# Convolution-attention hybrid on one core: attention steps at an even rate, layer 0 divided by token, the third convolution on VectorE, an earlier load of x, and the last feed-forward in step

## The chip, the core and the metric

The kernel runs on one core of a Trainium2 chip. The metric is the device time from the first to the last instruction, in microseconds (us). Before the change it is 7679.73 us, the median of three runs (7679.41 to 7688.48). The profile shown here is of an execution with a span of 7673.1 us. The engines are named as in the profile: PE (TensorE matmul) and PEld (its weight loads), DVE (VectorE), ACT (ScalarE), POOL (GpSimd) and SP (SyncE).

## The reference

The input x has 4 images of 128 channels and 64 x 64 = 4096 positions. Everything is fp32. Cut to what matters, this is computed:

```python
# layer 0, per image
e1 = prelu(w1 @ gn(x)); e2 = prelu(w2 @ gn(x)); asm = prelu(wa @ gn(x))      # 64, 64 and 128 channels
x  = x + einsum('nij,ncj->nci', softmax(einsum('nci,ncj->nij', e1, e2), axis=2), asm)
# layer 1, attention over 4096 tokens of 128 numbers, 16 heads of 8
t  = tokens(x); y = ln(t)
q  = qz_ring(y + rx)                      # products of cosines; q is query, key and value at once
c  = softmax(q @ q.T / sqrt(8)) @ q       # per head
x1 = ln(y + c @ w_comb.T + b) * g1 + be1
t  = t + ln(x1 + relu((cos(x1[:8]) * cos(ry)) @ w1.T + b1) @ w2.T + b2) * g2 + be2
# last layer: a recurrence over the tokens after a norm over all of them
W' = batchnorm(ln(t) @ W.T);  y_k = sigmoid(W'_k + y_{k-1} @ V.T);  out = t + y
```

In layer 0 the softmax runs over j, so each position i is divided by a sum of its own. In attention q serves as query and as key, so the score of (i, j) is also that of (j, i).

## The kernel before, in words

The images are worked one after the other. Each has three stages.

**First stage** (`first_stage`, `layer0`, `tokens`). x lies by channel, `xs` of 128 x 4096. After the group norm three 1x1 convolutions make e1, e2 and asmT. The first two are rectified by `prelu` (two Relu passes on ACT, L281 and L282, and one product on DVE, L283), the third one likewise. Then come 8 tiles `ic` of 512 positions i. For each the loop takes the 4096 positions j in 32 groups of 128, two groups (one `jp`) at a time: `scores` makes s (PE, L365), p = exp(s) (ACT, L373) and adds p to `total` (DVE, L378 and L381), and `weigh` multiplies asmT with p into one accumulator (PE, L388). `take` copies the accumulator (L400). `result` sums `total` over partitions with two matmuls by a matrix of ones (L406), inverts the 128 x 512 result (L408), multiplies (L409) and adds to xs (L412, POOL); it also keeps the least and greatest inverse for a check at the end (L416). All this is by channel.

Between two groups the loop calls `meanwhile`. It runs one step of a queue of generators: `tokens(im, i)`, which turns a finished tile of xs by TensorE transposes (L470) into tokens x0 and makes the layer norm x1 and q (L478 to L508), and splits q for the scores (L512 to L521). It also runs steps of the feed-forward of the image before, two tiles at a time. PE, ACT and DVE keep the order in which the program emits their instructions. Transposes and sums of this stage share a pool `ps_tok` of one PSUM bank. The last tile's generator, `tail`, goes on inside attention.

**Second stage** (`attention`). For each of 8 pairs of heads there are 4 blocks of 1024 queries. A step of the inner loop, a *turn*, takes 128 keys `jt`: PE makes scores for two heads (4 matmuls on row tiles, L800), ACT the exp e of 128 x 1024 per head (L809), and PE weighs the turn before with the queries' own values (L679). Since scores are symmetric, only part of the blocks of keys is met: the first two blocks have 24 turns, the other two 16. A turn off the diagonal (`off`) serves twice. Its e is *flipped* by DVE (STREAM_TRANSPOSE in 32 x 32 pieces, L648), ACT sums its rows (`accum_out`), and the flipped copies of four such turns make a group of 16 *mirror steps* (`mirror_step`, L661), whose end goes to `later` by L672 or L674. Of every three turns of a long block two are off the diagonal, of every two in a short block one.

How many mirror steps PE does in a turn is set by a credit. Each turn adds a rate, the sum is capped at 4, and whole steps are taken as far as a group is pending:

```python
credit = min(credit + (3.0 if off else 2.0), 4.0)
if at == 1:
    credit = 4.0
credit -= run_pending(turn, int(credit))
```

A group becomes pending at a turn that `run_flips` sets when it has emitted the group's last flip (L650); `run_flips` holds back a group as long as the group two before it has steps left (L642). The exp tiles e lie in a pool of 6 or, in two of five turns, in the space of xs, which is free then (`exps`). Near the end of the last block xs is needed for the next image: `upcoming` holds the load of x (`load_x`), its statistics and the rest of the norm, started at given turns `at` (L864) and after the last turn (L881). `finish` and its `mirrored` and `result` (L703 to L747) move a block's sums to tokens, mostly by small copies on POOL.

**Third stage** (`third_stage`). The feed-forward of an image (`feed_forward`, 8 tiles of 512 tokens as generators) is interleaved by `in_steps` with the next image's first stage. After the last image it stands alone: each step of the loop takes every active generator one step on, and at most 6 are active.

At the end the recurrence runs over 64 chunks side by side. Each of 64 + 16 steps is two matmuls and a Sigmoid for each of two halves (L1265, L1283, L1290). `add_tokens` adds results to t2 in 16 tiles on DVE after every 16 steps (L1273), and DMAs take the 16 tiles out (L1316).

Of the kernel before, what the change touches and what calls it, by code (L numbers as in the profile page):

```python
# [10 lines left out]
F32 = mybir.dt.float32  # L11
# [15 lines left out]
def kernel(  # L27
# [32 lines left out]
    P = 128  # L60
# [155 lines left out]
    ranges = const.tile([1, 2, N * NIC], F32, tag="ranges", name="ranges")  # L216
# [38 lines left out]

    def transposed(src, name, kind="ps_one"):

        pt = get(kind, name)
        for k in range(TG):
            nc.tensor.transpose(pt[:, ts(k, P)], src[:, k, :], ident)  # L260
        return pt
# [22 lines left out]

    def norm_stats(n, xs):
# [19 lines left out]
    def layer0(n, xs, xh, norm, shifted, done, meanwhile):  # L305
# [23 lines left out]
        for i in range(NIC // 2):  # L329
# [19 lines left out]
            y, z = mid_tile(f"ya{n}_{i}"), mid_tile(f"za{n}_{i}")  # L349
            prelu(asmT[:, ts(i, 2 * IC)].rearrange("p (a b) -> p a b", a=2), pc, y, z, (0.0, 0.0), aa_sb)  # L350
# [51 lines left out]
        def result(ic):  # L402
            total, taken = state.pop(ic), state.pop(("sum", ic))
            sm = get("ps_tok", f"sum{n}_{ic}")
            for j in range(2):
                nc.tensor.matmul(sm, ones, total[:, j, :], start=j == 0, stop=j == 1)  # L406
            inv = half_tile(f"inv{n}_{ic}")
            nc.vector.reciprocal(inv, sm)  # L408
            nc.vector.tensor_tensor(taken, taken, inv, ALU.mult)  # L409

            eng = nc.gpsimd if ic < NIC - 1 else nc.vector
            eng.tensor_tensor(xs[:, ts(ic, IC)], xs[:, ts(ic, IC)], taken, ALU.add)  # L412
            if not shifted:
                for k, op in ((0, ALU.min), (1, ALU.max)):
                    at = n * NIC + ic
                    nc.vector.tensor_reduce(ranges[:, k, at : at + 1], inv[0:1, :], AX.X, op)  # L416
            done(ic)


        before = []  # L420
        for ic in range(NIC):
            for jp in range(0, NP, 2):
                fresh = [(ic, j, scores(ic, j)) for j in (jp, jp + 1)]
                for i in range(2):
                    if before:
# [3 lines left out]
                        elif before[i][0] and before[i][1] == 0:  # L429
                            result(before[i][0] - 1)  # L430
                    meanwhile()
# [4 lines left out]
        result(NIC - 1)  # L436
# [26 lines left out]
    def tokens(im, i):  # L463


        n, q, cols = im["n"], im["q"], ts(i, IC)
        yield
        yield
        yield
        pt = transposed(blocks(im["xs"][:, cols]), f"pt{n}_{i}", "ps_tok")  # L470
        x0 = get("thalf", f"x0_{n}_{i}")
        nc.scalar.copy(x0, pt)
        nc.sync.dma_start(out=im["x0"][:, cols], in_=x0)
        yield
# [952 lines left out]
```

## Time and profile before

The stages of the profiled execution, by the first and last exp of layer 0 and attention (L373, L809) and the first matmul of the recurrence (L1265):

| stage | from (us) | to (us) | length (us) |
|---|---|---|---|
| layer 0, image 0 (with the start) | 0 | 447.1 | 447.1 |
| attention, image 0 | 447.1 | 1764.3 | 1317.2 |
| layer 0, image 1, beside a feed-forward | 1764.3 | 2317.0 | 552.7 |
| attention, image 1 | 2317.0 | 3638.8 | 1321.8 |
| layer 0, image 2, beside a feed-forward | 3638.8 | 4193.4 | 554.6 |
| attention, image 2 | 4193.4 | 5512.6 | 1319.2 |
| layer 0, image 3, beside a feed-forward | 5512.6 | 6063.5 | 550.9 |
| attention, image 3 | 6063.5 | 7384.5 | 1321.0 |
| last feed-forward | 7384.5 | 7568.1 | 183.6 |
| recurrence and output | 7568.1 | 7673.1 | 105.0 |

Attention is 69% of the span. Within it, a long block of image 1 (head pair 4, block 1) goes from 3034.4 to 3084.0 us, the short ones after it to 3116.3 and 3148.3. The groups of the costliest lines:

```profile
L809 ACT ACTIVATE e<-s 128x1024 f32<-128x1024 f32 x3104 | 3068.5, 1027 | 117.1 <-PE s L800 104.8
L648 DVE STREAM_TRANSPOSE t<-e 128x1024 f32<-128x1024 f32 x1872 | 2201.4, 1218 | 653.4 <-ACT e L809 635.8
L661 PE MATMUL misc<-t,mirror 128*32 128x128 f32 x49152 | 1817.9, 278 | 55.4 <-DVE later L672 27.6
```

Each row gives line, engine, operation, output and inputs with their shapes and how often, then the busy time in us and the mean of one in ns, then the engine's idle time just before these instructions and what ended most of it. Matmuls on different row or column tiles of PE overlap, so their busy time is that of their union, and an fp32 matmul is recorded twice.

### The profile page before, as it was taken

The numbers are of one execution on the slowest core, as the hardware profiler recorded it, in microseconds if no ns is written. First come the engines' busy times: TensorE is split into PE (matmuls) and PEld (weight loads), VectorE is DVE, ScalarE is ACT, GpSimd is POOL, SyncE is SP. The second block draws the span as 40 slices with busy tenths as digits, with TensorE's granted clock in tenths as the row PEclk, the third lists the DMA queues.
The fourth block names the chain that finished last, engine by engine and source line by source line (L and its number), as shares of the span: only waits on it lengthen the run. The fifth ranks groups of instructions, "written<-read, shape, count | busy, mean of one in ns | idle before, by whom it ended". The sixth has DMA issues, their size and how long they took to land. (4 is left out here: it accounts for less than half of the span.)

```text
span 7673.1 us, 211342 instructions
## 1 busy us (share of the span) xinstructions
PE 7342.2 (96%) x87566; PEld 3334.3 (43%) x87566; DVE 5561.2 (72%) x7344; ACT 6146.6 (80%) x9493; POOL 2769.3 (36%) x9796
## 2 busy tenths in 40 slices
PE   8999999999999999999899999999999999999976
PEld 3334444444444444444444444444444444444445
DVE  5777777776787777777678777777677877777754
ACT  4479999995448999999444999999844699999964
POOL 1134444343223433343323343444322334444341
PEclk9999999999999999999999999999999999999987
DMA  0010000000111000000011000000001100000012
GB/s 26 25 42 23 25 19 20 19 9 24 33 44 36 25 20 19 23 21 16 18 33 46 32 20 19 22 23 17 17 25 34 52 20 23 23 25 19 11 53 102
DMA packets 81501, 211.92 MB, mean 28 GB/s; under 512 B 8768, under 2 KB 8800, under 8 KB 79760
## 3 DMA queue, kind: packets, MB, share of 16 engines
q1 hardware_dynamic: 77312, 186.68, 7.1%
q8 instruction: 689, 11.29, 0.6%
q10 hardware_dynamic: 2016, 10.49, 0.3%
q14 instruction: 284, 2.33, 0.1%
q0 software_dynamic: 1200, 1.14, 0.1%
HBM read 141.65 MB, written 56.62 MB: 26 GB/s over the span
## 5 line engine op out<-in xcount | busy, mean ns | idle before, releaser
L809 ACT ACTIVATE e<-s 128x1024 f32<-128x1024 f32 x3104 | 3068.5, 1027 | 117.1 <-PE s L800 104.8
L648 DVE STREAM_TRANSPOSE t<-e 128x1024 f32<-128x1024 f32 x1872 | 2201.4, 1218 | 653.4 <-ACT e L809 635.8
L809 ACT ACTIVATE xs<-s 128x1024 f32<-128x1024 f32 x2016 | 1993.0, 1025 | 49.4 <-PE s L800 46.3
L661 PE MATMUL misc<-t,mirror 128*32 128x128 f32 x49152 | 1817.9, 278 | 55.4 <-DVE later L672 27.6
L679 PE MATMUL acc<-e,q_aug 128*32 128x512 f32 x12416 | 1700.9, 595 | 0.0
L648 DVE STREAM_TRANSPOSE t<-xs 128x1024 f32<-128x1024 f32 x1200 | 1413.2, 1218 | 357.8 <-ACT xs L809 346.0
L661 PEld LDWEIGHTS misc<-t,mirror 128*32 128x32 f32 x49152 | 1225.5, 110 | 609.1 <-issue 450.9
L800 PEld LDWEIGHTS s<-queries,keys 32*128 32x128 f32 x10240 | 502.7, 181 | 2154.4 <-issue 1712.8
L715 POOL COPY own<-o 32x36 f32<-32x36 f32 x2048 | 428.6, 209 | 2768.7 <-DVE o L707 2688.8
L800 PE MATMUL s<-queries,keys 32*128 32x512 f32 x10240 | 1312.5, 495 | 11.0 <-ACT e L809 8.8
L679 PE MATMUL acc<-xs,q_aug 128*32 128x512 f32 x8064 | 1148.2, 595 | 0.0
L388 PE MATMUL acc<-p,asmT 128*128 128x512 f32 x2048 | 975.1, 610 | 0.0
L373 ACT ACTIVATE p<-s 128x1024 f32<-128x1024 f32 x512 | 497.0, 1022 | 519.9 <-PE s L365 512.7
L381 DVE TENSOR_TENSOR total<-total,p 128x1024 f32<-128x1024 f32 x448 | 578.0, 1290 | 243.8 <-ACT p L373 220.4
L618 POOL COPY mirror<-q 32x128 f32<-32x128 f32 x2048 | 595.2, 291 | 94.7 <-PE misc L661 6.8
L388 PEld LDWEIGHTS acc<-p,asmT 128*128 128x128 f32 x2048 | 364.2, 191 | 543.8 <-issue 541.5
L365 PE MATMUL s<-e,e 64*128 64x512 f32 x2048 | 531.6, 639 | 4.6 <-ACT p L373 3.0
L734 POOL COPY other<-turned 32x64 f32<-32x64 f32 x2048 | 472.2, 231 | 95.7 <-DVE turned L727 9.9
L679 PEld LDWEIGHTS acc<-e,q_aug 128*32 128x32 f32 x12416 | 390.1, 110 | 91.3 <-issue 42.8
L809 ACT ACTIVATION_READ_ACCUMULATOR e<-s 128x1 f32 x1872 | 388.7, 208 | 0.0
L679 PEld LDWEIGHTS acc<-xs,q_aug 128*32 128x32 f32 x8064 | 259.0, 109 | 112.0 <-issue 55.0
L365 PEld LDWEIGHTS s<-e,e 64*128 64x128 f32 x2048 | 181.9, 192 | 278.2 <-issue 251.1
(237 smaller groups left out, 4901.8 us busy)
## 6 DMA issues: line engine op xcount, KB each, us to landing
keys<-parts_dram SPq DMA_DIRECT2D x256, 256.0 KB
queries<-parts_dram SPq DMA_DIRECT2D x1024, 32.0 KB
fx<-x_dram SPq DMA_DIRECT2D x64, 256.0 KB
x_dram<-x SPq DMA_DIRECT2D x56, 256.0 KB
xs<-in_x_dram SPq DMA_DIRECT2D x16, 512.0 KB
t_dram<-t2T SPq DMA_DIRECT2D x32, 256.0 KB
t2s<-t_dram SPq DMA_DIRECT2D x16, 512.0 KB
parts_dram<-high SPq DMA_DIRECT2D x28, 256.0 KB
```

The costliest lines, as they stand in the source:

```text
L365: nc.tensor.matmul(s[:, j, :], e2[rows, ts(2 * jp + j, P)], e1[rows, ts(ic, IC)], start=True, stop=True,)
L373: nc.scalar.activation(p, s, AF.Exp)
L381: nc.vector.tensor_tensor(state[ic], state[ic], p, ALU.add)
L388: nc.tensor.matmul(state["acc", ic], asmT[:, ts(2 * jp + j, P)], p[:, j, :], start=jp == 0 and j == 0, stop=jp == NP - 1 and j == 1,)
L618: nc.gpsimd.tensor_copy(wv[ts(a, 32), s, :, :, ts(a, D)], own[ts(s, 32)])
L648: nc.vector.transpose(group["e"][h][:, k, :], es[h])
L661: nc.tensor.matmul(state["acc"][ts(2 * h + x, 32), :], state["w"][:, QT * (s // 4) + TG * x + s % 4, h, :], state["e"][h][:, :, ds(IC * x ...
L679: nc.tensor.matmul(it["acc"][ts(2 * h + x, 32), :], it["qa"][:, ds((2 * it["jt"] + h) * V, 32)], it["e"][h][:, ts(x, IC)], start=it["first ...
L715: nc.gpsimd.tensor_copy(own[ts(s, 32), ts(x, 4), h, :], ov[ts(2 * h + x, 32), s, :, 0:V])
L734: nc.gpsimd.tensor_copy(to[ts(k, 32), h], tv[ts(2 * h + x, 32), k])
L800: nc.tensor.matmul(ss[h][:, x, :], keys[jt // QT].bitcast(F32R)[r, cols], queries[b].bitcast(F32R)[r, :], start=True, stop=True,)
L809: nc.scalar.activation(es[h], ss[h].rearrange("p x c -> p (x c)"), AF.Exp, scale=1.0 / math.sqrt(D), accum_out=denom[:, slot, jt, h : h + ...
```

## The change

The change has five parts.

1. *Attention.* The rates at which mirror steps are handed out become those at which they come: 2.9 and 2.2 in long blocks, 2.2 and 1.9 in short ones. A group is pending one turn later. The last tile's generator starts a turn later, one step a turn; as long as it runs, its tokens stand in part of xs, and `exps` uses the pool in place of that part.
2. *Layer 0 by token.* The sums over partitions are made by token and not by channel: the ones matrix is cut to 32 columns, so that a sum of 128 columns goes to each of four column tiles, a DVE transpose and a small inversion give one inverse per token, and the product with the inverse and the addition to x are made in one DVE instruction on the transposed tile. x itself is transposed first. The check of the inverses uses all of them, kept in `inverses`.
3. *Third convolution.* It is rectified by two DVE instructions that read PSUM, in place of two on ACT and one on DVE.
4. *x sooner.* The next image's x is loaded at turn 2 of the last block in place of turn 8; the end of its norm comes after the last mirror steps.
5. *Ends.* In the last feed-forward all 8 tiles are active together, and ACT does their normalisations. In the recurrence the additions follow steps 16, 32, 48, 60 and 64.

The diff, cut to its core:

```diff
+    def normalise_act(dst, src, mv, rstd, n_tiles, name):
+        less = stats.tile([P, n_tiles], F32, tag=f"less{n_tiles}", name=f"less_{name}")
+        nc.vector.scalar_tensor_tensor(less, mv[:, :, 0], -1.0, rstd, ALU.mult, ALU.mult)
+        for k in range(n_tiles):
+            at = slice(k, k + 1)
+            nc.scalar.activation(
+                dst[:, k, :], src[:, k, :], AF.Identity, bias=less[:, at], scale=rstd[:, at]
+            )
...
+    def prelu_vector(dst, src, minus, minus_slope):
+        nc.vector.tensor_scalar(minus, src, 0.0, minus_slope, ALU.min, ALU.mult)
+        nc.vector.scalar_tensor_tensor(dst, src, 0.0, minus, ALU.max, ALU.subtract)
...
-            y, z = mid_tile(f"ya{n}_{i}"), mid_tile(f"za{n}_{i}")
-            prelu(asmT[:, ts(i, 2 * IC)].rearrange("p (a b) -> p a b", a=2), pc, y, z, (0.0, 0.0), aa_sb)
+            to = asmT[:, ts(i, 2 * IC)].rearrange("p (a b) -> p a b", a=2)
+            prelu_vector(to, pc, mid_tile(f"za{n}_{i}"), aa_sb)
...
-        def result(ic):
-            total, taken = state.pop(ic), state.pop(("sum", ic))
-            sm = get("ps_tok", f"sum{n}_{ic}")
-            for j in range(2):
-                nc.tensor.matmul(sm, ones, total[:, j, :], start=j == 0, stop=j == 1)
-            inv = half_tile(f"inv{n}_{ic}")
-            nc.vector.reciprocal(inv, sm)
-            nc.vector.tensor_tensor(taken, taken, inv, ALU.mult)
...
                             take(before[i][0])
-                        elif before[i][0] and before[i][1] == 0:
-                            result(before[i][0] - 1)
-                    meanwhile()
+                            begin(before[i][0], state)
+                    meanwhile(2 if ic == NIC - 1 else 1)
...
-    def tokens(im, i):
+    def tokens(im, i, sums):
...
+        pt = transposed(blocks(im["xs"][:, cols]), f"px{n}_{i}", "ps_tok")
+        x0 = im["xs"][:, cols] if last else get("thalf", f"x0_{n}_{i}")
         nc.scalar.copy(x0, pt)
+        yield
+        total, taken = sums.pop(i), sums.pop(("sum", i))
+        ps = get("ps_tok", f"sum{n}_{i}")[:, 0:P]
+        tv = total.rearrange("p j (k c r) -> p j c k r", c=4, r=32)
+        for j in range(2):
+            for c in range(4):
+                nc.tensor.matmul(
+                    ps[ts(c, 32), :],
+                    ones[:, 0:32],
+                    tv[:, j, c],
...
+                )
+        by_token = small.tile([P, P], F32, tag="sums", name=f"sums{n}_{i}")
+        nc.vector.transpose(by_token, ps)
...
+        nc.vector.reciprocal(inv, by_token.rearrange("p (k r) -> p k r", k=TG)[:, :, 0])
+        if not last:
+            yield
+        pt = transposed(blocks(taken), f"pt{n}_{i}", "ps_tok")
+        if not last:
+            yield
+        for k in range(TG):
+            at = ts(k, P)
+            nc.vector.scalar_tensor_tensor(
+                x0[:, at], pt[:, at], inv[:, k : k + 1], x0[:, at], ALU.mult, ALU.add
+            )
...
-                    pending.append((turn + 1, group["steps"], group["block"]))
+                    pending.append((turn + 2, group["steps"], group["block"]))
...
-            if k < 0 or last:
+            if k < 0 or last or (k and tail):
...
-                    es = exps(name, end_of_all and at >= QT)
+                    es = exps(name, end_of_all and at >= 2)
...
-                    credit = min(credit + (3.0 if off else 2.0), 4.0)
+                    rates = (2.9, 2.2) if len(behind[b]) == 2 else (2.2, 1.9)
+                    credit = min(credit + rates[0 if off else 1], 4.0)
                     if at == 1:
-                        credit = 4.0
+                        credit = max(credit, 3.0)
...
-                    for _ in range(3 if tail and turn == 2 else 1):
-                        if tail and turn > 1 and next(tail, tail) is tail:
-                            tail = None
-                            rest()
-                    if end_of_all and at in (QT, QT + 6) and upcoming:
+                    if tail and turn > 2 and next(tail, tail) is tail:
+                        tail = None
+                        rest()
+                    if end_of_all and at in (2, QT + 6) and upcoming:
...
-        for f in upcoming:
-            f()
         while flips or pending:
             run_flips(TG)
             run_pending(turn + 2, 16)
+        for f in upcoming:
+            f()
...
-            while len(own) > 1:
-                step_first(own)
+            *own, tail = own
+            for g in own:
+                for _ in g:
+                    pass
             while step_late():
                 pass
-        return own.pop()
+            while not next(tail):
+                pass
+        return tail
...
-            step = in_steps(feed_forwards(im, final), 1, 6)
+            step = in_steps(feed_forwards(im, final), 1, NTG)
...
-                if t >= 0 and t % 16 == 15 and t + 1 < L:
-                    add_tokens(t - 15, t + 1)
+                if t + 1 in added:
+                    add_tokens(*added[t + 1])
...
-        add_tokens(L - 16, L)
+        add_tokens(L - 4, L)
```

## Prediction

> **What bounds the kernel now.** I read the page's busy shares, a table of windows cut at the stages, the timeline of TensorE in two attention blocks, and the waits of one attention stage.
>
> The page's engine shares:
> ```profile
> PE 7342.2 (96%) x87566; PEld 3334.3 (43%) x87566; DVE 5561.2 (72%) x7344; ACT 6146.6 (80%) x9493; POOL 2769.3 (36%) x9796
> ```
> PE looks full, but a pipelined PE always does, so the stages decide. Windows (length, then busy us of each engine, granted clock, DMA):
> ```profile
> 27.00:434.00 407.00, 400.50 (x1201) 160.09 (x1202) 272.26 (x358) 182.30 (x192) 47.90 (x57) 1.00 0.06 19
> 1777.00:2308.00 531.00, 497.21 (x1729) 227.04 (x1730) 394.94 (x772) 244.96 (x279) 151.29 (x179) 0.96 0.10 32
> 2317.00:3639.00 1322.00, 1302.84 (x19846) 576.48 (x19846) 979.84 (x1020) 1278.07 (x2054) 525.52 (x2213) 1.00 0.07 23
> 7385.00:7568.00 183.00, 104.33 (x657) 76.57 (x649) 109.35 (x423) 44.39 (x73) 97.06 (x156) 0.68 0.19 69
> ```
> Rows one and two, layer 0 without and with a feed-forward beside it, are PE's. Row three, one of four attentions, has PE and ACT both nearly full: they trade the lead turn by turn. In row four, the last feed-forward, nobody is full: latency.
>
> PE in a long attention block, then in a short one (start, us):
> ```profile
> 2703.01 0.51 PE L800 MATMUL s<-queries,keys 32*128 32x512 f32 x4
> 2703.45 0.86 PE L661 MATMUL misc<-t,mirror 128*32 128x128 f32 x24
> 2704.13 1.04 PE L679 MATMUL acc<-e,q_aug 128*32 128x512 f32 x8
> 2705.10 0.51 PE L800 MATMUL s<-queries,keys 32*128 32x512 f32 x4
> ...
> 2706.77 0.52 PE L800 MATMUL s<-queries,keys 32*128 32x512 f32 x4
> 2707.47 1.08 PE L661 MATMUL misc<-t,mirror 128*32 128x128 f32 x32 [0.18 <-DVE later L672]
> ```
> ```profile
> 3099.80 0.51 PE L800 MATMUL s<-queries,keys 32*128 32x512 f32 x4
> 3100.24 1.08 PE L661 MATMUL misc<-t,mirror 128*32 128x128 f32 x32
> ...
> 3111.89 0.51 PE L800 MATMUL s<-queries,keys 32*128 32x512 f32 x4
> 3112.33 1.27 PE L679 MATMUL acc<-e,q_aug 128*32 128x512 f32 x8
> 3113.53 0.62 PE L800 MATMUL s<-queries,keys 32*128 32x512 f32 x4
> 3114.09 1.63 PE L679 MATMUL acc<-e,q_aug 128*32 128x512 f32 x8
> ```
> A mirror step shows as 8 records. A PE turn is scores 0.44 (2703.01 to 2703.45), k steps 0.03 + 0.218k (3 steps: 0.68), weighing 0.97 (2704.13 to 2705.10): 1.44 + 0.218k, so 2.09 for three steps, 1.87 for two. ACT's floor, from the closest starts of L809, is 1.99 us for a turn with row sums (off the diagonal) and 1.81 without. Long block (24 turns, 16 off, 64 steps): PE 24 x 1.436 + 64 x 0.218 = 48.4, ACT 16 x 1.99 + 8 x 1.81 = 46.3. Short block (16 turns, 8 off, 32 steps): PE 29.9, ACT 30.4. Measured from block start to block start: 49.5 to 49.7 and 32.0 to 32.3. Two losses explain this. Long: a batch's first step starts 0.70 us after its scores instead of 0.44, because the flips it reads are only just done: about 0.27 x 4 batches = 1.1. Short: the 16 steps of a batch run as 4,2,3,2,3,2 and then two turns have none; PE then sets the pace in six turns and ACT in two.
>
> The waits of an attention stage (2381 to 3600) name it:
> ```profile
> PEld misc L661 <- DVE later L672: 14.5, 29, 0.5
> PEld misc L661 <- DVE later L674: 8.0, 16, 0.5
> PE misc L661 <- DVE later L672: 5.4, 29, 0.2
> ```
>
> **What the Trainium skill says.** "Perfetto Trace Analysis", Identifying the Most-Contended Engine: matmul busy share is no measure of nearness to roofline. The trace agrees: PE shows 98.5% in attention although short blocks lose 1.6 us of 32. "TensorE: Matmul & The Clock Gate", Part 3 (row/col tiling): matmuls on different column tiles run at once. The trace agrees: four L661 matmuls, of 272 ns each, start every 0.109 us. "VectorE: DVE Perf Modes", Why PSUM operands drop a tier: fp32 from PSUM runs at 1x. Here L519 (PSUM, 512 elements) takes 687 ns, L230 (SBUF, one source) 422. "ScalarE: Activation LUTs", Table sets: copy, relu and identity are in every set; all 116 table loads here stand at Sin, Exp and Sigmoid lines, none at Copy or Relu.
>
> **The change, part by part.**
>
> *Attention rates and the start one turn later.* Counting the credit rule turn by turn gives, before, 3,3,1,4,3,2 steps per six turns of a long block and the 4,2,3,2,3,2,0,0 above (both are what the trace shows); after, 2,4,2,3,3,2 and nearly all 2. Nothing is added. The batch's first step has 2 us of slack over its flips, so the 1.1 us wait goes; the two-buffer rule of L642 never holds a flip in the count. Long: 49.6 to 48.6 (PE floor plus 0.2). Short: two steps cost PE 1.87, below ACT's mean 1.90, so ACT sets it: 32.1 to 30.7 (floor plus 0.3). Per head pair 2 x 1.0 + 2 x 1.4 = 4.8; x 8 pairs x 4 images = **-154**. Bounds: half of it (-77), or both floors exactly (-176).
>
> *Layer 0 divided by token.* Removed on PE per tile: two full sums, four passes of 0.43 = 1.72, and the transposes of xs with their wait for POOL (L412), 1.00 by the timeline. Added: px and pt, 0.44 each like pq (155.68 to 156.12), and eight 32-column sums, 4 rounds of 0.109 plus switching = 0.55. Net -1.3. DVE loses 3.35 (L408) + 0.69 + 1.33 and gains a transpose (0.25, between L727's 410 ns for twice the size and L674's 258), a reciprocal (0.24 as L741) and four multiply-adds (0.26 to 0.36 each, L674 and L503): -3.5, which hides under PE. New waits: px, sum, pt and pq share the one ps_tok bank; behind a waiting one on PE queue the scores and weighings, and ACT and everything else wait for those. They stand a `meanwhile` (2.8 us) apart, evacuations take 0.3 to 1.5, so without feed-forward nothing waits: image 0 -9. Beside the feed-forward DVE runs late (PE's longest wait for it there is 4.7 us), so I keep -6 for images 1 to 3: **-26** (bounds +20, -42).
>
> *Third convolution.* ACT loses 2 x 1.02 per pair of tiles; DVE goes from 1.29 to two PSUM reads of 1.2 to 1.4. PE takes 3.9 per pair, so it hides; Exp's table load (1.28) moves off the first score: **-4** (bounds +8, -8).
>
> *Tail.* Image 1's first block takes 63.6 against 49.5, the others 58.7, 61.1, 62.8. In image 1 ACT stands 8.3 us at 2332 to 2341 because PE's first mirror step waits for flips that DVE began only at 2323, after reciprocal, product, add and ranges (2316.5 to 2322.6). These leave that place and the step comes one turn later; two Sin/Exp loads and the pq transposes stay, and the shorter exps pool (6 buffers, reused after 3 turns) costs a little: -4 an image, **-16** (bounds +8, -30).
>
> *x sooner.* The load lands by 1756, the statistics run at 1763.8 behind the flips: hidden already. The reordered end lets PE do its last 16 steps during the statistics, but the next convolutions stand behind POOL's chain until 1795 (L741 on DVE's queue), which is not shortened: **0** (bounds +3, -8).
>
> *Last feed-forward.* Six tiles run from 7417 to 7517, the last two alone to 7564. With eight in step the second, half-empty phase goes. DVE gives 96 normalisations (37 us) to ACT for 24 small products, ACT pays 96 x about 0.35 (L1290, L239) on 44 of 183 us busy. 100/6 less 4 of DVE per tile = 12.7; 8 x 12.7 = 102 to 130 us from 7417: **-32** (bounds -12, -48).
>
> *Recurrence.* The output DMA (8.4 MB, about 405 GB/s, 20.7 us) starts after the first final add, 7647.7. Now 16 adds of 12 tokens (about 0.40 each from L1273's 0.50 pitch for 16) start at 7643.1 and hold DVE until 7649.5: **+2**.
>
> Sum: -154 - 26 - 4 - 16 - 32 + 2 = -230; 7679.7 - 230 = **7450**.
>
> **Rivals.**
> - *Half the pacing (a wait takes the other's place).* PE and ACT have only 1.5 turns of scores between them; turns of 4 steps (2.31) may still let ACT idle, or misc wait elsewhere. For: ACT waits for scores 28.7 us per attention now. Against: the sums per six turns are even. -77 instead of -154: 7527.
> - *All floors met.* -176 - 42 - 30 - 48 - 8 + 2: about 7378.
> - *ps_tok stalls PE (slower).* If pt and pq each waited 4.7 us in 24 tiles (+226), layer 0's saving were gone and pacing brought half: 7680 + 226 - 77 - 32 - 16 = 7781. For: PE is in order and DVE is late there. Against: 4.7 us is the longest of eight waits above 1.7 in image 1, and DVE gets 3.5 us lighter per tile.
>
> **How the numbers follow.** As summed 0.70; half pacing 0.17; all floors 0.06; slower 0.07 (a little of it ends within 0.2%). 7385 to 7550 leaves out the stalls and the best end. Faster 0.92, same 0.02, slower 0.06.
>
> **What would show it.** Block starts 48.4 to 48.8 and 30.4 to 31.0 apart; no L672 wait before L661; layer-0 tiles of image 0 at 46.3 instead of 47.55 us; last feed-forward 140 to 165 us; output 2 us later. Wrong if short blocks stay at 32, if PE waits for ps_tok (L260, after a DVE transpose) grow, or if ACT stalls in the first block for want of exps.

## The result, and the profile after

The changed kernel takes 7469.64 us (median, 7459.55 to 7473.21) against 7683.31 us before (four runs, 7679.41 to 7688.48; the 7679.73 ahead of the prediction is the median of three of them): a ratio of 0.9719, interval 0.9703 to 0.9736. That is 213.7 us less, where 229.7 were predicted. By stages of the two profiles (cut at the same instructions as in the table of before), in us:

| stage | before | after | difference |
|---|---|---|---|
| layer 0, image 0 | 447.1 | 447.3 | +0.2 |
| attention, image 0 | 1317.2 | 1277.5 | -39.7 |
| layer 0, image 1 | 552.7 | 546.5 | -6.2 |
| attention, image 1 | 1321.8 | 1275.1 | -46.7 |
| layer 0, image 2 | 554.6 | 554.5 | -0.1 |
| attention, image 2 | 1319.2 | 1275.3 | -43.9 |
| layer 0, image 3 | 550.9 | 550.3 | -0.6 |
| attention, image 3 | 1321.0 | 1274.2 | -46.8 |
| last feed-forward | 183.6 | 164.7 | -18.9 |
| recurrence and output | 105.0 | 106.2 | +1.2 |

The differences sum to -201.6. The 12 us up to the measured 213.7 are mostly one oddity of the profile of before: its third convolution of image 0 had PE's full clock, which 11 of the 14 profiles of this study do not have (shown below). Four fifths of the gain are in attention, where three quarters were forecast. Layer 0 gave nearly nothing, and the last feed-forward three fifths of what was forecast.

The page's engine shares after:

```profile
PE 7212.8 (97%) x88078; PEld 3317.1 (44%) x88078; DVE 5435.5 (73%) x7364; ACT 6104.6 (82%) x9557; POOL 2718.0 (36%) x9768
```

The shares have hardly moved though 214 us are gone: they could not have told it before, and do not now. The windows that answer to the four of before (start and end, length, then busy us and instructions of PE, PEld, DVE, ACT and POOL, granted clock, DMA share, GB/s):

```profile
27.00:430.00 403.00, 397.42 (x1296) 164.43 (x1298) 245.29 (x378) 173.32 (x183) 32.77 (x65) 0.97 0.06 21
1738.00:2263.00 525.00, 491.33 (x1844) 227.29 (x1844) 374.14 (x793) 238.72 (x273) 155.15 (x215) 0.95 0.10 34
2272.00:3546.00 1274.00, 1270.34 (x19846) 568.28 (x19840) 976.63 (x1018) 1264.18 (x2052) 519.28 (x2194) 1.00 0.07 23
7201.00:7365.00 164.00, 106.24 (x661) 79.77 (x651) 81.39 (x354) 81.55 (x170) 94.62 (x156) 0.71 0.21 78
```

In the third row PE has 4 us without work in 1274 and ACT 10; before it was 19 and 44 in 1322. So both engines now have work for nearly the whole stage. In the fourth row DVE has gone from 109 to 81 us and ACT from 44 to 82.

PE in a long attention block after (timeline: start, us, instruction):

```profile
2678.53 0.51 PE L833 MATMUL s<-queries,keys 32*128 32x512 f32 x4
2678.97 0.64 PE L693 MATMUL misc<-t,mirror 128*32 128x128 f32 x16
2679.43 1.04 PE L711 MATMUL acc<-e,q_aug 128*32 128x512 f32 x8
2680.41 0.50 PE L833 MATMUL s<-queries,keys 32*128 32x512 f32 x4
2680.84 0.64 PE L693 MATMUL misc<-t,mirror 128*32 128x128 f32 x16
...
2682.27 0.51 PE L833 MATMUL s<-queries,keys 32*128 32x512 f32 x4
2682.70 1.08 PE L693 MATMUL misc<-t,mirror 128*32 128x128 f32 x32
```

and in a short one:

```profile
3059.77 0.65 PE L693 MATMUL misc<-t,mirror 128*32 128x128 f32 x16
...
3061.64 0.64 PE L693 MATMUL misc<-t,mirror 128*32 128x128 f32 x16
...
3063.53 0.64 PE L693 MATMUL misc<-t,mirror 128*32 128x128 f32 x16
```

Eight records are a step. Every batch, also one of four steps (2682.70), now starts 0.43 us after its scores; before, a batch's first took 0.70. In the short block nearly every turn has two steps. Blocks start 48.2 to 48.3 (long) and 30.7 to 31.0 us (short) apart; before 49.5 to 49.7 and 32.0 to 32.3. The groups of the page:

```profile
L842 ACT ACTIVATE e<-s 128x1024 f32<-128x1024 f32 x3144 | 3096.7, 1036 | 25.3 <-PE s L833 15.2
L693 PE MATMUL misc<-t,mirror 128*32 128x128 f32 x49152 | 1867.8, 279 | 12.5 <-DVE later L704 11.4
```

The last column but one is idle time before the group: for the exps it fell from 117.1 to 25.3, for the mirror steps from 55.4 to 12.5. And 11.4 of these 12.5 are new: three waits of 3.8 us, at the ends of images 0 to 2 (below).

### The profile page after: what moved, and what is told of

It reads as the page before. It is cut to its first block, busy times and chain, and to the rows that moved or that the text cites. A ratio compares the mean times of both kernels' runs of the same rounds, so it can differ in the third digit from the quotient of the medians.

```text
span 7471.5 us, 212466 instructions
## 1 busy us (share of the span) xinstructions
PE 7212.8 (97%) x88078; PEld 3317.1 (44%) x88078; DVE 5435.5 (73%) x7364; ACT 6104.6 (82%) x9557; POOL 2718.0 (36%) x9768
## 5 line engine op out<-in xcount | busy, mean ns | idle before, releaser
L842 ACT ACTIVATE e<-s 128x1024 f32<-128x1024 f32 x3144 | 3096.7, 1036 | 25.3 <-PE s L833 15.2
L842 ACT ACTIVATE xs<-s 128x1024 f32<-128x1024 f32 x1976 | 1958.5, 1036 | 17.5 <-PE s L833 5.5
L693 PE MATMUL misc<-t,mirror 128*32 128x128 f32 x49152 | 1867.8, 279 | 12.5 <-DVE later L704 11.4
L711 PE MATMUL acc<-e,q_aug 128*32 128x512 f32 x12576 | 1683.9, 595 | 0.0
L680 DVE STREAM_TRANSPOSE t<-xs 128x1024 f32<-128x1024 f32 x1176 | 1375.4, 1214 | 352.1 <-ACT xs L842 351.5
L693 PEld LDWEIGHTS misc<-t,mirror 128*32 128x32 f32 x49152 | 1200.2, 110 | 623.5 <-issue 598.8
L711 PE MATMUL acc<-xs,q_aug 128*32 128x512 f32 x7904 | 1055.7, 594 | 0.0
L711 PEld LDWEIGHTS acc<-e,q_aug 128*32 128x32 f32 x12576 | 396.1, 110 | 33.6 <-ACT e L842 18.9
L842 ACT ACTIVATION_READ_ACCUMULATOR e<-s 128x1 f32 x1896 | 406.5, 214 | 0.0
```

Of the source, the lines that this page charges most:

```text
L680: nc.vector.transpose(group["e"][h][:, k, :], es[h])
L693: nc.tensor.matmul(state["acc"][ts(2 * h + x, 32), :], state["w"][:, QT * (s // 4) + TG * x + s % 4, h, :], state["e"][h][:, :, ds(IC * x ...
L711: nc.tensor.matmul(it["acc"][ts(2 * h + x, 32), :], it["qa"][:, ds((2 * it["jt"] + h) * V, 32)], it["e"][h][:, ts(x, IC)], start=it["first ...
L842: nc.scalar.activation(es[h], ss[h].rearrange("p x c -> p (x c)"), AF.Exp, scale=1.0 / math.sqrt(D), accum_out=denom[:, slot, jt, h : h + ...
```

## The experiments

Four runs take the attention apart or take back the doubled steps of layer 0, four undo one part each, four follow what these showed. Times are medians; the kernel before gave 7682 to 7687 beside them.

### Pacing alone, and its two halves

```diff
-                    pending.append((turn + 1, group["steps"], group["block"]))
+                    pending.append((turn + 2, group["steps"], group["block"]))   # delay
...
-                    credit = min(credit + (3.0 if off else 2.0), 4.0)
+                    rates = (2.9, 2.2) if len(behind[b]) == 2 else (2.2, 1.9)
+                    credit = min(credit + rates[0 if off else 1], 4.0)
...
-                        credit = 4.0
+                        credit = max(credit, 3.0)
```

Each is the kernel before with both edits, with the first alone, or with the other two alone.

> The kernel before with the attention pacing alone (new rates, credit of at least 3 at the second turn, groups pending one turn later). Theory A, pacing carries attention: the four attentions lost 177 us in the changed kernel, 18 of them in the first block of each image, where other parts of the change act too; so about -159 here, 7683 - 159 = 7524 (7512 to 7536), long blocks 48.2 to 48.6, short ones 30.8 to 31.1, first blocks within 2 us of before. Theory B, the pacing needs the rest of the change (the tail's later start, the exps pool): under -120, above 7563.

> The kernel before with only the later start (a group is pending two turns on, old rates). Counting the credit rule: long blocks get 2,4,2,3,3,2 steps, exactly as in the changed kernel; short blocks get 2,4,2,3,2,3 and then 2 and 0 or 0 and 0: nearly as before. Theory A, long blocks lose their time to the wait for flips and short ones to the turns without steps: long 48.3, short 31.7 to 32.2; 64 long blocks x 1.25 = -80, 7603 (7585 to 7615). Theory B, the even rates do it in both: 7670 to 7690.

> The kernel before with only the rates and the credit of at least 3 (groups pending one turn on, as before). Counting: long blocks get 4,2,3,3,2,2 with the batch still begun in the turn after its last flip; short blocks mostly 2 with a 4 and one 0. Theory A: long blocks stay at 49.5 to 49.7, short ones go to 31.0 to 31.4; 64 short x 1.0 = -64, 7619 (7605 to 7635). Theory B, the rates carry all of it: long 48.3 and about 7530. Theory C, without the delay nothing is gained: above 7665.

| kernel | us | ratio (interval) | long blocks | short blocks |
|---|---|---|---|---|
| before | 7685.7 | | 49.5, 49.7 | 32.2, 32.0 |
| later start alone | 7570.1 | 0.9848 (0.9832 to 0.9865) | 48.2, 48.3 | 31.8, 31.6 |
| rates alone | 7628.8 | 0.9927 (0.9910 to 0.9943) | 49.3, 49.6 | 31.3, 31.4 |
| both | 7527.2 | 0.9789 (0.9773 to 0.9806) | 48.2, 48.3 | 30.8, 31.0 |

Pacing alone brings 158 us of the 214. Theory A had 159; only the first blocks moved a little more than it allowed (by -3.0 to +0.4). The two halves act in different blocks. The later start does all of the long ones (-1.35) and a third of the short ones (-0.4); the rates do the rest of the short ones and next to nothing in the long ones (-0.15). The page's groups say it in two lines each. With the later start alone:

```profile
L809 ACT ACTIVATE e<-s 128x1024 f32<-128x1024 f32 x3104 | 3068.6, 1026 | 28.3 <-PE s L800 14.9
L661 PE MATMUL misc<-t,mirror 128*32 128x128 f32 x49152 | 1828.4, 278 | 9.9 <-POOL mirror L553 8.5
```

With the rates alone:

```profile
L809 ACT ACTIVATE e<-s 128x1024 f32<-128x1024 f32 x3104 | 3057.8, 1036 | 95.7 <-PE s L800 84.1
L661 PE MATMUL misc<-t,mirror 128*32 128x128 f32 x49152 | 1854.4, 278 | 77.1 <-DVE later L672 49.3
```

The wait ahead of the mirror steps goes with the start one turn later and even grows (55.4 to 77.1) with the rates alone. So the wait was not one for the number of steps but for the moment at which the batch begins. The expectation for the later start (7585 to 7615) was missed by 15 us: it had 1.25 for a long block and nothing for a short one; 64 x 1.35 + 64 x 0.4 = 112 against the 116 measured. The rates alone fell into their theory A (7605 to 7635). The even rates were thought to be the greater part of the saving, and are the smaller. The halves, 116 and 57 us, sum to 173, 15 more than the two together: some 10 are the 0.15 in long blocks, which is not won twice, and the rest is small beside what runs differ by.

### One step a turn in layer 0's last tile

```diff
-                    meanwhile(2 if ic == NIC - 1 else 1)
+                    meanwhile(1)
```

> The changed kernel with one step of the token generators, not two, in each turn of layer 0's last tile. There this tile takes 54.7 us in images 1 to 3 beside a feed-forward (46.2 before the change) and 46.9 in image 0 (45.0 before). A generator has 16 stops and a tile 16 turns, so one step a turn is just enough. Theory A, the doubled steps push a Sin and its DVE chain in front of the feed-forward's last copy on ACT and so make PE wait 4.2 us there, and bring more waits: the last tile of images 1 to 3 falls to 46 to 50 us, attention starts at most 2 us later, together -9 to -20: 7455 (7445 to 7463). Theory B, what is not done in the last tile is done after it: the last tile falls, but the time to the first exp of attention grows by as much, and the total stays within 4 us of 7470.

7450.5 us, 0.9690 (0.9674 to 0.9706): 19 us faster than the changed kernel, inside theory A. The tiles of layer 0 tell what happened. Images 1 to 3, from one `take` to the next: the first six pitches summed to 382.2, 379.1 and 380.4 us before and to 365.9, 368.0 and 368.5 after, 11 to 16 us less, more than forecast. The seventh went from 46.2 to 54.7, 54.7 and 55.2, and here it is 45.5. This is the place in the changed kernel (timeline, with the idle time before an instruction and what ended it):

```profile
2238.07 0.68 DVE L237 SCALAR_TENSOR_TENSOR r<-r 128x512 f32<-128x512 f32 x1
2238.79 0.72 ACT L239 ACTIVATE r<-r,half_pi 128x512 f32<-128x512 f32 x1 [4.05 <-DVE r L237]
2239.42 1.05 ACT L1101 COPY last<-pl 128x512 f32<-128x512 f32 x1
2240.53 2.07 PE L1042 MATMUL pwx<-last,WT_sb 128*128 128x512 f32 x2 [4.21 <-ACT last L1101]
```

ACT's queue holds the Sin of a token tile ahead of the feed-forward's copy. The Sin waits 4 us for DVE's chain, the copy, whose input was ready since 2234.6, waits behind it, and PE, the engine that bounds the stage, waits 4.2 us for the copy. DVE, where the chain begins, had no pause (8.7 of the 9.0 us ahead of the Sin are busy): the Sin's inputs stand among its other work.

The wait has a second price. From 2239.1 to 2245.9 us PE's granted clock is 0.50. Two instructions of this stretch in the changed kernel (timeline of PE alone), then the same two with one step a turn:

```profile
2240.53 2.07 PE L1042 MATMUL pwx<-last,WT_sb 128*128 128x512 f32 x2 [4.21 <-ACT last L1101]
2242.53 3.65 PE L380 MATMUL s<-e,e 64*128 64x512 f32 x8
```

```profile
2237.12 1.02 PE L1042 MATMUL pwx<-last,WT_sb 128*128 128x512 f32 x2
2238.07 1.99 PE L380 MATMUL s<-e,e 64*128 64x512 f32 x8
```

These two take 2.7 us longer. With the wait of 4.2 and one of 1.55 for the sums (DVE, L489) that makes 8.5 of the 9.3 us that the tile is longer. All 21 last tiles of images 1 to 3 in the seven profiles with doubled steps have the wait of 4.2 us and 6.8 us of half clock that begin before its end; the nine with one step a turn have neither, and after the waits of 1.7 us in image 0 the clock stays at 1.00. With one step a turn PE waits for no other engine in the last tile.

Not all comes free: the first attention block of images 1 to 3 takes 59.7 to 60.0 us in place of 55.4 to 56.8. A part of the doubling's use was there, but it cost 9 us to gain 3 to 4.

### The norm's end ahead of the last mirror steps

```diff
+        for f in upcoming:
+            f()
         while flips or pending:
             run_flips(TG)
             run_pending(turn + 2, 16)
-        for f in upcoming:
-            f()
```

> The changed kernel with the end of the next image's norm back ahead of the last mirror steps. In the trace of the changed kernel PE's last 16 steps wait 3.8 us for a copy that DVE does behind the statistics, the norm's two small matmuls stand behind them, and POOL waits 2.5 us for the norm's variance ahead of its long chain of copies; the convolutions stand behind that chain. Theory A: the convolutions of images 1 to 3 get back 2.4 us each (start of the first to start of the third 31.2 to 28.8): -7, 7462. Theory B, the delay comes from the longer tail or from x loaded sooner: no change, 7468 to 7472.

The changed kernel at the end of image 0's attention (last exp: 1724.8):

```profile
1729.14 0.37 DVE L306 BATCH_NORM_AGGREGATE gmv<-gst 128x2 f32<-128x48 f32 x1
1729.43 0.23 DVE L704 COPY later<-misc 128x128 f32<-128x128 f32 x1
1729.71 5.37 PE L693 MATMUL misc<-t,mirror 128*32 128x128 f32 x128 [3.80 <-DVE later L704]
1735.01 0.38 PE L309 MATMUL pg<-gmv,grp 128*128 128x1 f32 x2
1736.90 0.56 POOL L225 TENSOR_TENSOR r_g<-v_g,minus_half 128x1 f32<-128x1 f32 x1 [2.53 <-DVE v_g L223]
```

The last 16 steps cannot run during the statistics: they wait for the copy L704 of the batch before them, which DVE has queued behind the statistics. The norm's matmuls follow, and POOL is 2.5 us late. With the order turned back, the time from the first to the third convolution falls in images 1 to 3 from 31.2, 34.0 and 31.2 to 29.1, 31.8 and 29.1 us, as theory A had it. The total does not show it: 7469.9 us (7460.8 to 7472.8), 0.9721 (0.9705 to 0.9737). Seven us in all are within what single runs differ by (12 us here). So the delay is shown in the trace, and its worth in the time is not settled.

### The last feed-forward: who normalises, and how many in step

```diff
-            if final:
+            if False:                                                  # normalise on DVE
                 normalise_act(blocks(dst), blocks(src), mv, rstd, TG, f"{name}{n}_{i}")
...
-            step = in_steps(feed_forwards(im, final), 1, NTG)
+            step = in_steps(feed_forwards(im, final), 1, 6)            # six in step
```

Each run makes one of these edits.

> The changed kernel with the last feed-forward's normalisations back on DVE, all eight tiles still in step. One on ACT took 0.484 us there, 96 of them 46 us, where the prediction had 0.35 and 34; on DVE one took 0.37 to 0.49. Theory A, DVE limited the stage before and the move is what frees it: the stage grows from 164.7 to 174 to 182 us. Theory B, the move is worth nothing because ACT is as slow as DVE, and the gain is from eight in step: 160 to 168.

> The changed kernel with at most six tiles of the last feed-forward in step, normalisations on ACT. Theory A, the phase with the last two tiles alone returns (47 us before, some 12 of them saved by eight in step): 174 to 185 us in place of 164.7. Theory B, eight in step bring nothing since one engine or another is full anyway: 162 to 168.

DVE with eight in step: 7477.8 us, 0.9730 (0.9714 to 0.9746). ACT with six: 7490.7, 0.9749 (0.9732 to 0.9765). The stage, with before and after:

| | six in step | eight in step |
|---|---|---|
| normalised on DVE | 183.6 (before) | 167.7 |
| normalised on ACT | 188.6 | 164.7 (after) |

The stage's window with DVE and eight, then with ACT and six (columns as above):

```profile
7192.00:7359.70 167.70, 105.15 (x664) 78.06 (x662) 110.98 (x426) 43.49 (x73) 96.89 (x156) 0.69 0.21 76
```

```profile
7185.50:7374.00 188.50, 106.50 (x663) 77.16 (x661) 86.34 (x354) 82.73 (x170) 95.35 (x156) 0.71 0.19 68
```

The first run fell into its theory B (the move is worth nothing, 160 to 168), the second beyond its theory A (174 to 185): both theories A were too kind to the move to ACT. Eight profiles with the changed kernel's last feed-forward have 162.9 to 165.0 us in this stage and four with the old one 181.7 to 183.6, so differences of 3 us stand out of that spread. The move takes 23 to 29 us of work from DVE and puts 38 on ACT, and the stage gains 3 us of it with eight tiles in step and loses 5 with six. Eight in step alone is worth 16. This stage, in which no engine is over two thirds full, paid little for lighter work on one engine and much for more tiles under way. The groups of the stage in the changed kernel show the price on ACT (last two figures ahead of the idle time: busy us, mean ns):

```profile
L262 ACT ACTIVATE q<-q,less_u,r_u 128x128 f32<-128x128 f32 x32 | 14.0, 485 | 16.2 <-DVE less_u L259 16.2
L262 ACT ACTIVATE v<-v,less_v,r_v 128x128 f32<-128x128 f32 x32 | 13.3, 482 | 14.0 <-DVE less_v L259 13.5 <-DVE zk L231 0.4
```

The Trainium skill has this price: "ScalarE: Activation LUTs", What ACT_TABLE_LOAD costs, gives 186 ns + 0.833 ns an element and says that "each `[128,1]` pointer operand adds ≈ 93 ns". With 128 elements and two such operands (bias and scale) that is an estimate of 186 + 107 + 186 = 479 ns; the trace has 482 and 485. The prediction took 350 from rows with other operands.

### The third convolution back on ACT

```diff
-            prelu_vector(to, pc, mid_tile(f"za{n}_{i}"), aa_sb)
+            y, z = mid_tile(f"ya{n}_{i}"), mid_tile(f"za{n}_{i}")
+            prelu(to, pc, y, z, (0.0, 0.0), aa_sb)
```

> The changed kernel with the third convolution rectified by two ACT passes and one DVE product, as before. Theory A, it is hidden as the prediction has it, but for the Exp table load: from the start of the third convolution to the first p 0.5 to 1.5 us longer in each image, +2 to +6 in all, 7472 to 7476; the granted clock of 0.5 in image 0's third convolution stays, since three kernels with the old rectification showed it too. Theory B, DVE's two reads of PSUM hold the convolution back: 2 us shorter in each image, 7462.

7470.7 us (7464.1 to 7476.1), 0.9719 (0.9703 to 0.9735): no difference that the time can show. In the trace of images 1 to 3 the time from the third convolution to the first p is 27.1, 27.5 and 27.2 us, in place of 24.3, 26.1 and 24.2. Much of that is PE's clock: with the instructions of the changed kernel, the two runs on the last feed-forward take 22.8 us at a granted clock of 0.78, 24.2 at 0.72 and 26.0 at 0.67, and this run had 0.68 to 0.69. Time multiplied by clock is 18.6 to 19.0 us here and 17.4 to 17.6 there, so at this clock the two passes on ACT cost an estimated 1.7 us more up to the first p, a little above theory A's 0.5 to 1.5. But the first tile gives half or more of it back: from the first p to the first `take` this run needs 55.2 us, as before the change, and the changed kernel 56.1 to 56.5. What is left of the move to DVE is under 1 us an image. In image 0 this run can't be read against the changed kernel, because of PE's clock; at full clock on both sides, before against the kernel with six tiles in step, the way to the first p is 19.0 and 16.7 us, to the first `take` 64.6 and 64.2. The window from 46 to 72 us, which holds that convolution, in the changed kernel and then in the kernel with six tiles in step (the two differ only in the last feed-forward):

```profile
46.00:72.00 26.00, 26.00 (x84) 16.81 (x84) 11.16 (x9) 3.13 (x3) 0.00 (x0) 0.61 0.00 1
```

```profile
46.00:72.00 26.00, 24.07 (x108) 13.15 (x109) 16.01 (x13) 6.97 (x7) 0.00 (x0) 1.00 0.00 1
```

The same instructions at a granted clock of 0.61 and of 1.00: the convolution takes 26.4 us and 16.7. Of the 14 profiles of this study three have 1.00 here, among them that of before, and eleven 0.56 to 0.80, among them three kernels with the old layer 0 (0.61 to 0.67). So the change did not bring the lower clock. It is why image 0 shows no gain in the table: against those three (456 to 458 us up to the end of layer 0) the changed kernel's 447.3 is 9 to 11 us less. At full clock on both sides the kernel with six in step ends layer 0 at 437.9, 9.2 us ahead of the 447.1 of before. Forecast were 9 for image 0 and 1 for the convolution.

### The two ends of attention later, the statistics sooner, and all together

The changed kernel stands once more in the second convolution of images 1 to 3:

```profile
1758.60 0.25 DVE L773 RECIPROCAL inv<-own 128x16 f32<-128x16 f32 x1 [8.30 <-POOL own L769]
1761.58 2.07 PE L339 MATMUL pcb<-q,w_sb 128*128 128x512 f32 x2 [7.54 <-ACT za L292]
```

DVE's queue waits for POOL with an inverse that the feed-forward needs only much later; behind it stand the convolution's products, and behind these ACT and PE.

```diff
             def meanwhile(steps=1):
-                if before and before["left"]:
+                calls[0] += 1                                        # starts at 0
+                if calls[0] > 8 and before and before["left"]:        # ends later
                     before["left"].pop(0)()
...
-                    if end_of_all and at in (2, QT + 6) and upcoming:
+                    if end_of_all and at in (2, QT + 2, QT + 6) and upcoming:   # statistics sooner
```

> The changed kernel with the last two ends of an attention (each an inverse and a product on DVE behind POOL's copies) put on the queues at the ninth and tenth stop of the next first stage, not at the first and second. In the changed kernel PE and ACT stand 7.5 us in the second convolution of images 1 to 3, because DVE's queue waits at such an inverse for POOL. Theory A, POOL's chain holds the convolutions only through DVE's order: start of the first to start of the third convolution 31.2 to about 24 us, -22 in all, 7448 (7440 to 7456). Theory B, DVE or the feed-forward behind it takes its place: less than -8, above 7462.

> The changed kernel with the next image's statistics at turn 10 of the last block (x is loaded at turn 2) and the end of its norm at turn 14, where the changed kernel has the statistics at turn 14 and the rest after the last mirror steps. Theory A, x sooner then bears fruit: PE's last 16 steps no longer wait 3.8 us behind the statistics, the norm is ready when attention ends, and the first convolution starts 7 to 10 us after the last exp in place of 13.3; -9 to -18 in all: 7455 (7450 to 7462). Theory B, the 5.4 us of statistics delay the flips of the last block and it gets as much longer: within 4 us of 7470.

Ends later: 7454.9 us, 0.9703 (0.9688 to 0.9718), 15 us faster than the changed kernel. The wait is gone: first to third convolution 22.4, 28.0 and 24.6 us, together 21 less, as expected. But the third convolution takes 3.2, 1.7 and 5.0 us longer: in images 1 and 3 PE waits 4.8 and 4.0 us there (0.6 in the changed kernel), in image 2 its clock was lower (0.63 against 0.67). So theory A has the mechanism, and a part of its size was given back there.

Statistics sooner: 7468.5 us, 0.9721 (0.9706 to 0.9736), no gain. The first convolution starts 6.3 to 7.3 us after the last exp in place of 13.3 to 14.2, as theory A had it; the last block of attention takes 36.1 to 36.5 us in place of 31.1, which is theory B's price. The price is not paid through the flips alone, however:

```profile
1726.87 0.35 PE L317 MATMUL pv<-tv,grp 128*128 128x1 f32 x2 [4.52 <-DVE tv L315]
...
1727.78 1.94 ACT L842 ACTIVATE e<-s 128x1024 f32<-128x1024 f32 x2 [4.89 <-PE s L833]
...
1748.36 4.29 PE L339 MATMUL pca<-q,w_sb 128*128 128x512 f32 x6 [5.65 <-DVE q L327]
```

PE now waits in attention for the norm's small DVE operations, which DVE has queued behind 4.6 us of flips; the next scores stand behind that matmul, and ACT stands too. In the convolution PE waits 5.65 us for a product of DVE's, which stands behind a transpose that waits 9.3 us for POOL. From the last exp to the first p images 1 to 3 still win 4.6, 8.4 and 2.6 us, and the last blocks lose 5.0, 5.4 and 5.4.

> The changed kernel with three edits together: one token step a turn in layer 0's last tile, the two ends of attention at the ninth and tenth stop, statistics at turn 10 and the norm at turn 14. Theory A, they act at different places and add up: -19 (measured alone) -22 -13 = -54, 7416 (7405 to 7430). Theory B, the second and third share one wait (whichever is last, POOL's chain or the norm): 7430 to 7445.

> The changed kernel with one token step a turn in layer 0's last tile, the two ends of attention at the ninth and tenth stop, and the end of the norm ahead of the last mirror steps (statistics at turn 14 as in the changed kernel). It differs from the run with the statistics at turn 10 in that the last block of attention is not lengthened by a norm that PE waits for (31.1 us in place of 36.5), while the first convolution starts later (about 13 us after the last exp in place of 6.5). Theory A, what the early statistics won at the start of the convolutions they lost in the last block: within 5 us of 7433. Theory B, the early norm is worth its price: above 7438. Theory C, it costs more than it brings: below 7428.

With one step a turn, ends later and statistics sooner: 7432.7 us (7428.9 to 7441.2), 0.9679 (0.9666 to 0.9692). With the norm's end ahead of the mirror steps in place of the early statistics: 7430.6 us (7426.8 to 7437.9), 0.9674 (0.9660 to 0.9687). The two can't be told apart, as theory A of the last run had it; the attentions of images 0 to 2 are 3 to 5 us shorter in the second and the convolutions start 6 us later. The first run fell into theory B's span: -19 and -15 from the single runs make -34, the early statistics add some 3. They are 37 and 39 us faster than the changed kernel, from which they differ in the order of instructions alone, and 250 and 251 faster than the one before.

## Why the prediction was right

7450 was forecast and 7469.6 measured, inside 7385 to 7550, and the likeliest case was the one that came. The greatest term was right in its mechanism; the smaller ones were right in part, and one by luck. Term by term, in us:

| step of the prediction | forecast | measured | read from |
|---|---|---|---|
| attention pacing | -154 | -158 | time of pacing alone (its attention stages alone: -166) |
| tail, first block | -16 | -11 | attention stages after, -177, less the -166 |
| layer 0 by token and third convolution | -30 | -24 | image 0 -10 at like clock; images 1 to 3 -14 (-7 by stages, where the +7 of the next row is included) |
| x sooner and the reordered end | 0 | +7 | first to third convolution, trace alone |
| last feed-forward | -32 | -19 | stage |
| recurrence | +2 | +1 | stage |

With -166 for the pacing the column sums to -212, and -213.7 was measured.

*Pacing: right, with the two parts a little differently sized.* Long blocks gained 1.35 where 1.0 was forecast, and short ones 1.2 where it was 1.4; the errors cancel in part. The prediction gave the long blocks to the wait for flips and the short ones to the uneven counts. The two halves run alone confirm the first wholly and the second for two thirds: in short blocks too, a third went with the later start. The floor of 48.4 for PE in a long block was 0.2 too high. The idle sums bear it out: ACT's wait for scores and the mirror steps' wait fell together, so no wait took another's place, and the rival of half the pacing falls. (The 28.7 us of ACT's wait in that rival are of the window from 2381 to 3600; with the first block it is 40.) The bound of -176 for both floors does not follow from the prediction's own floors: 2 x 1.2 and 2 x 1.7 make 5.8 a head pair, so -186, and the rival with all floors met would stand at 7368.

*Layer 0: a term was left out.* "Net -1.3" per tile is what image 0 shows exactly (pitch 46.28 us, 46.3 forecast), and beside a feed-forward six tiles saved 11 to 16 us, where 6 were forecast for the whole image (-9 and three times -6 make -27, not the -26 of the sum). 4.5 to 5.0 of these are waits of PE for the feed-forward's t (DVE, L980 and L1022), which fell from 7.8 to 8.1 us an image to 3.1 to 3.3 with the lighter DVE; the prediction had no term for them. What it also left out is the last tile: the change makes two token steps in each of its turns, which the diff shows and neither its five parts nor the prediction name. Against before that cost 8.5 to 9 us an image beside a feed-forward (1.9 in image 0), by a Sin put ahead of a copy on ACT and the half clock after the wait. The run with one step a turn shows it. The prediction's new waits for the ps_tok bank did come, but small (PE ahead of pt, "DVE sums L489": 1.9 to 2.4 us an image, 0.3 to 0.4 with one step a turn), and the slower rival with 4.7 us twice a tile falls.

*Third convolution: -4 forecast, less than that in the trace and nothing that the time shows.* The price was right: 1.28 and 1.22 us for the two DVE instructions (L297, L298), where 1.2 to 1.4 was said. The lines that it was read from did not show it, however: L519 has two sources and L230 one, and L409, with two sources in SBUF, takes 692 ns beside the 687 of L519 from PSUM. What was missed is that the first tile gives back half or more of what the convolution wins.

*The reordered end: 0 forecast, 2.4 us lost in each of images 1 to 3.* The step "lets PE do its last 16 steps during the statistics" was wrong: these steps wait for a copy that DVE does after the statistics. The trace shows it; the time does not resolve it.

*Last feed-forward: the step that was mis-sized.* The prediction divided a lighter DVE by the number of tiles ("100/6 less 4 of DVE per tile"), as if DVE set the pace. The move to ACT was worth 3 us, not 4 a tile, and an ACT normalisation cost 0.48 us, not 0.35. The other reason, that eight in step remove the half-empty phase, carried 16 of the 19.

*Tail: right in sum, by luck.* The first blocks of images 0 to 3 took 58.7, 63.6, 61.1 and 62.8 us before, 56.1, 61.4, 58.1 and 63.2 with pacing alone and 59.4, 56.8, 56.7 and 55.4 after. That of image 0 can't be used: with the attention of the changed kernel untouched it was 55.7 and 57.6 in the two runs on the last feed-forward. In images 1 to 3 the sum is 182.7 with pacing alone, 168.9 after, and 179.4 with one step a turn. So 10 of the 14 us are bought by the doubled steps of layer 0's last tile, which the prediction doesn't name, and some 3 are left for the causes that it names.

## What to carry to other kernels

Where work is handed out by a budget, first look at when a batch may begin and only then at how much is done at a time: a start one turn later, past the producer's end, brought 116 us, the even rates alone 57. In a stage of interleaved generators, price each added step by what stands behind it on each in-order queue; a step that is cheap on every engine can still put 4 us between two engines that are not concerned, and the half clock that followed this wait made it dearer. Before a stage's difference is put down to an edit, compare the granted clock of both sides. And where no engine is near full, as in the last feed-forward here, put more independent tiles under way before moving work from one engine to another.

## What the runs showed of the hardware that was not expected

PE's granted clock in one and the same stretch (third convolution of image 0, fp32) was 1.00 in three profiles and 0.56 to 0.80 in eleven, with kernels whose instructions there are identical on both sides: 16.7 against up to 28.1 us. In images 1 to 3 that convolution never had the full clock (0.59 to 0.80 in all 14 profiles), and with the same instructions its time followed the clock: 22.8 us at 0.78 and 26.0 at 0.67 in the two runs on the last feed-forward, where PE had next to no pause in it (0.5 to 0.7 us). One profile's stage of 20 us can so be 10 us off; what decides the clock there stays open.

In layer 0's last tile it was regular: with each of 21 waits of PE of 4.2 us came 6.8 us at a clock of 0.50, which begin 0.5 to 1.7 us before the wait ends, and with none of the seven waits of 1.7 us in image 0.

An ACT Identity of 128 x 128 with bias and scale from SBUF takes 482 to 485 ns, while the same normalisation on DVE took 337 to 590 in the stage beside other work, so here neither is clearly the cheaper engine.
